# Four hand-written step lists in a graph-attention kernel, put into another order

## The chip, the cores and the metric

The kernel runs on one core of a Trainium2 chip. A time is the device time of one execution in microseconds (us); for a kernel it is the median of the runs shown. The engines are called as in the profile: PE (TensorE's matmuls), PEld (its weight loads), DVE (VectorE), ACT (ScalarE), POOL (GpSimd) and SP (SyncE, which here only issues DMAs).

## What is computed

Two graph-attention layers over 128 batches of 128 nodes with 512 features, all in float32, each with a residual and a layer norm:

```python
# layer 0: 8 heads of 64, masked by adj
q, k, v = x @ Wq + bq, x @ Wk + bk, x @ Wv + bv
logits  = einsum('bqhd,bkhd->bhqk', q, k) / sqrt(64)
attn    = softmax(where(adj > 0, logits, -1e9))
o       = einsum('bhqk,bkhd->bqhd', attn, v)
x       = layernorm(x + relu(o @ Wo + bo))
# layer 1: one head, additive scores, softmax over the senders (axis=1)
Wh = x @ W
e  = leaky((Wh @ a1)[:, :, None] + (Wh @ a2)[:, None, :])
x  = layernorm(x + leaky(softmax(where(adj > 0, e, -9e15), axis=1) @ Wh))
```

## The kernel before

**The order is written out by hand.** The kernel switches the framework's own scheduling off (`tc.manual_schedule`): every engine does its instructions in the order in which the program issues them, and that order stands in strings of tokens. `BEGIN` starts, `PLAN` ends; between them a loop runs t = 6 to 123, 118 times, one batch each, and plays the list `STEADY[t % 4]`. Four lists, 0 to 3, so make one round over a group of four batches, and the loop makes 29.5 rounds. Each token calls one method, which issues a few instructions to one or more engines. In a list, therefore, only the order of tokens that share an engine (or wait for each other) means anything.

**Products.** Q, K and V of a group of four batches (lines 605 to 791) and the products with Wo and W (`pair_product`, line 793, for two batches) use Strassen's scheme: seven products p1 to p7 instead of eight, with sums of blocks before and after. The group products use it twice, one inside the other. The tokens:

- `h`: one of the seven products of a Q, K or V chain, 3 or 4 matmuls of 128x128 (line 681). What has to be read from its PSUM bank goes into two waiting lists: `a` takes the next from the first (a copy by ACT, lines 694 and 697), `d` from the second (an addition by DVE with one operand in PSUM, line 715).
- `k`, `k.v`: one of the 24 sums of two SBUF blocks per group that end the chains (line 731), by POOL or by DVE.
- `q`: one DMA of streamed weights (`w_n`, line 634); four buffers.
- `m.sum.N`, `p.sum.N`, `s.sum.N` (lines 523 to 526): the outer sums before a product, by POOL. `i.s1a` ... `i.s4b` (line 500): the inner ones, by POOL, with `.v` by DVE.
- `z.*`: the product with Wo of two batches, its residual and norm (`LayerZero`); `w.*`: that with W (`LayerOne`). `p1`..`p7` are matmuls (line 801, 0.86 us each), `t0 t2 t3` and `w.c21` copies by ACT, the other `c..` additions by DVE, `by bw` ACT's fill of a bank with the bias.

**Attention of layer 0** (`Softmax`, lines 855 to 980). `f` is the even batch of a pair, `s` the odd one. In lists 0 and 2 both are started: `scores` (line 875) is eight matmuls of 64 rows, which use two halves of the array in turn, and fills two PSUM banks. `add.0 add.1` (889) and `reduce` (898) are DVE's, `exp` (909) and `divide` (923) ACT's, head by head, `reciprocals` DVE's. In lists 1 and 3 both end: `store` (930) writes the weights to DRAM and `fetch` (936) reads them back in another layout, `transpose` (942) is DVE's, `attend` (955) eight matmuls with 64 columns, `copy` (970) four ACT instructions that free its bank.

**Layer 1's attention.** `v.*` and `e.*` (`Senders`, `Edge`; `e.product` is the matmul of line 1211, `e.copy` the ACT instruction of line 1218 that frees its bank and needs that the earlier `n.store`, line 1234, has left the same buffer); `n.*` is the end of the batch before: residual (1221), statistics (1003), `rstd` (POOL, 1009 and 1011), `apply` (DVE, 1024) and the store of the output. `g.*` finishes layer 0's norm of the pair before and fetches it back (421) turned for layer 1.

**Banks.** All matmul results but those of `h` share a pool of five PSUM banks:

```python
ps_mm = ctx.enter_context(tc.tile_pool(name="ps_mm", bufs=5, space=PSUM))
ps_st = ctx.enter_context(tc.tile_pool(name="ps_st", bufs=1, space=PSUM))
```

A new result takes over a bank of the five from an earlier one; PE waits until that one's last reader is done.

Of the kernel before, what the change touches and what calls it, by code (L numbers as in the profile page):

```python
# [70 lines left out]

STEADY = {
    0: """
        k.v n.residual q f.scores h h m.masks m.sum.0 m.sum.1 m.sum.2 m.sum.3 k.v g.apply.0
        q k.v w.p1 f.add.0 f.add.1 g.store.0 e.turn_blocks a e.add m.cast w.t0 s.scores
        f.reduce w.p6 f.exp.0.1 f.exp.2.3 d w.t2 f.exp.4.5 f.exp.6.7 d n.stats s.add.0
        f.reciprocals.0 s.add.1 e.maxima f.reciprocals.1 s.reduce w.p5 h n.rstd w.p7 w.p2 h
        h m.residuals q g.fetch_both a w.t3 e.exp q q w.c22 w.c11 f.divide.2.3 s.exp.2
        f.divide.0.1 a f.divide.6.7 e.divide w.p4 w.p3 h h h w.c21 s.exp.5 v.senders
        f.divide.4.5 s.exp.0.1 a i.s1a.v n.apply d s.exp.6.7 s.exp.3.4 q n.store v.store  # L80
        f.store g.transpose.1 g.transpose.0 i.s3a.v e.product h m.x_pair i.s2a i.s1b m.turn
        d k.v m.mask i.s3b.v a s.reciprocals.0 s.reciprocals.1 w.c12 d i.s2b.v k.v e.copy
        v.fetch
    """,
    1: """
        p.sum.0 z.by n.residual h z.p2 h k h a s.divide.5.6 i.s4a a f.fetch z.p1 h h d
        n.stats n.rstd k.v m.turn e.turn_blocks s.divide.3.4 s.divide.7 s.divide.0.1
        s.divide.2 n.apply z.bw z.t0 h z.p6 z.t2 a m.cast z.p5 z.p7 k k k h z.c11
        f.transpose z.t3 e.add d z.p4 s.store z.c22 a z.p3 h h m.mask e.maxima z.c21 s.fetch
        n.store q e.exp a a d z.stats.1 e.divide i.s4b h e.product h f.attend z.c12 e.copy  # L90
        f.copy p.sum.1 z.rstd.1 p.sum.2 z.apply.1 s.transpose q z.stats.0 d s.attend s.copy
        p.sum.3 z.rstd.0 k k s.sum.2 s.sum.0 s.sum.1 k s.sum.3 m.x_one z.store.1
    """,
    2: """
        f.scores n.residual g.apply.0 w.p1 f.add.1 f.add.0 s.scores e.turn_blocks w.t0 e.add
        w.p6 f.reduce w.t2 w.p2 h w.p7 m.turn k.v k.v f.exp.4.5 f.exp.6.7 f.exp.0.1 k.v w.p5
        h w.t3 a f.exp.2.3 n.stats f.reciprocals.1 w.c22 e.maxima w.c11 f.reciprocals.0
        e.exp f.divide.2.3 n.rstd w.p4 h w.c21 v.senders a d n.apply f.divide.4.5
        f.divide.6.7 f.divide.0.1 e.divide s.add.0 s.add.1 d h w.p3 q g.store.0 m.residuals
        m.masks h e.product h h a a g.fetch_both m.x_one n.store v.store s.reduce  # L100
        g.transpose.0 w.c12 q f.store v.fetch q m.cast d g.transpose.1 m.mask s.exp.5 e.copy
    """,
    3: """
        s.exp.3.4 z.by s.exp.6.7 k.v n.residual n.stats p.sum.0 h f.fetch a s.exp.2 z.p2
        z.p1 h h s.exp.0.1 z.t0 n.rstd q k.v z.p6 p.sum.1 p.sum.2 s.reciprocals.0
        s.reciprocals.1 d s.divide.5.6 a s.divide.0.1 s.divide.7 s.divide.3.4 h
        e.turn_blocks n.apply d z.t2 s.divide.2 m.cast m.turn h a a h z.p7 h h d m.mask
        z.c11 z.bw e.add a z.t3 k k k e.maxima f.transpose k z.p5 q e.exp h h z.p4 h a a d
        z.c22 s.store q q e.divide z.c21 s.fetch z.p3 h d z.stats.1 z.c12 k h n.store
        e.product z.rstd.1 p.sum.3 z.apply.1 d z.stats.0 h h f.attend s.transpose a e.copy a  # L110
        s.attend f.copy s.copy k z.rstd.0 s.sum.0 q z.store.1 s.sum.2 s.sum.1 m.x_one
        s.sum.3
    """,
}

# [1640 lines left out]
```

## Time and profile before

| | us |
|---|---|
| median of 3 runs (2304.18 to 2306.5) | 2305.35 |
| the profiled execution | 2304.29 |
| its span | 2302.5 |
| PE busy | 2265.1 (98%) |
| DVE busy | 2076.6 (90%) |
| ACT busy | 1661.2 (72%) |
| POOL busy | 1443.9 (63%) |
| DMA queue, share of 16 engines' span | 80.3% |

The table's busy times are unions over the span. A matmul's end is modelled, so a busy PE isn't proof of a PE at its peak: for PE, the distance from one start to the next is the number to read. The granted clock of TensorE is full throughout (0.998).

### The profile page before, as it was taken

How to read it: one execution, taken by the hardware profiler on the slowest of the kernel's cores; microseconds unless marked ns; L12 is line 12 of the kernel's file. 1: busy time of each engine (PE TensorE's matmuls, PEld its weight loads, DVE VectorE, ACT ScalarE, POOL GpSimd, SP SyncE). 2: the span in 40 equal slices, each digit the busy share in tenths (PEclk: the TensorE clock that was granted, in tenths of full speed). 3: DMA queues.
4: the chain of work that ended last, by engine and by line, in shares of the span. 5: the costliest groups of instructions: out<-in, count | busy, mean ns of one | idle time of the engine just before them, and what ended most of it. 6: DMA issues, size and time to landing. Idle time of an engine off the chain costs nothing.

```text
span 2302.5 us, 52596 instructions
## 1 busy us (share of the span) xinstructions
PE 2265.1 (98%) x17228; PEld 2013.5 (87%) x17228; DVE 2076.6 (90%) x4199; ACT 1661.2 (72%) x5955; POOL 1443.9 (63%) x1723
## 2 busy tenths in 40 slices
PE   9899999999999999999999999999999999999998
PEld 5889888888898898888988988889889889888885
DVE  5889999999999999999999999999999999999977
ACT  3767767777677677776776776877767767768786
POOL 2666676666766666666667666666666676666656
PEclk9999999999999999999999999999999999999999
DMA  9988888878888888888878888788888788888764
GB/s 234 278 232 233 235 236 243 243 233 228 242 234 251 235 230 237 242 243 239 234 228 243 233 246 241 233 233 242 242 240 237 225 246 235 247 236 233 214 214 144
DMA packets 516593, 540.79 MB, mean 235 GB/s; under 512 B 100568, under 2 KB 394336, under 8 KB 516320
## 3 DMA queue, kind: packets, MB, share of 16 engines
q1 hardware_dynamic: 516000, 537.17, 80.3%
q8 instruction: 137, 2.24, 0.4%
q14 instruction: 136, 1.11, 0.2%
q10 hardware_dynamic: 320, 0.26, 0.0%
HBM read 388.96 MB, written 148.31 MB: 233 GB/s over the span
## 4 chain that ended last, share of the span: by engine, by line
PE 58%; DVE 19%; DMA 9%; POOL 6%; SPq 3%; issue 3%; ACT 2%; DVEq 0%; POOLq 0%; ACTq 0%
PE p_y L801 14%; PE st_y L681 13%; PE lg L875 6%; PE p_w L801 6%; PE st_w L681 6%; PE st_x L681 5%; DVE pa L942 4%; PE p_x L801 4%; DMA w_n<-wv 3%; PE p_oT L955 3%; DVE arena L1047 3%; DVE cells L715 2%; DVE st L1003 2%; PE p_h L1211 2%; DVE arena L1024 2%
## 5 line engine op out<-in xcount | busy, mean ns | idle before, releaser
L909 ACT ACTIVATE pa<-pa,nmax 128x128 f32<-128x128 f32 x1000 | 391.6, 397 | 8.7 <-DVE nmax L898 8.7
L923 ACT ACTIVATE pa<-pa,rs 128x128 f32<-128x128 f32 x1000 | 329.2, 397 | 14.4 <-DVE rs L919 14.3
L1009 POOL TENSOR_SCALAR ve<-mv 128x1 f32<-128x1 f32 x256 | 77.6, 303 | 289.5 <-DVE mv L1005 228.4
L694 ACT COPY cells<-st_y 128x384 f32<-128x384 f32 x279 | 131.7, 472 | 101.4 <-PE st_y L681 98.9
L1024 DVE TENSOR_SCALAR arena<-arena,mv,rstd 128x512 f32<-128x512 f32 x239 | 185.5, 776 | 14.3 <-POOL rstd L1011 14.1
L909 ACT ACTIVATION_READ_ACCUMULATOR pa<-pa,nmax 128x1 f32 x1000 | 194.6, 195 | 0.0
L970 ACT ACTIVATE arena<-p_oT,b_cols 128x128 f32<-128x128 f32 x504 | 144.1, 371 | 58.9 <-PE p_oT L955 54.8
L523 POOL TENSOR_TENSOR x1S<-x1T 128x256 f32<-128x256 f32 x62 | 57.6, 929 | 204.2 <-DVE mf L853 204.2
L1011 POOL TENSOR_TENSOR rstd<-ve,mhalf 128x1 f32<-128x1 f32 x256 | 160.8, 628 | 21.3
L1003 DVE BATCH_NORM_STATS2 st<-arena 128x6 f32<-128x512 f32 x248 | 168.0, 678 | 1.2
L889 DVE TENSOR_TENSOR pa<-lg,mf 128x512 f32<-128x512 f32 x250 | 161.2, 675 | 4.6 <-PE lg L875 4.6
L942 DVE STREAM_TRANSPOSE pa<-paz 128x1024 f32<-128x1024 f32 x125 | 154.5, 1236 | 8.5 <-DMA paz<-pa_dram 6.1
L955 PE MATMUL p_oT<-pa,out_V 128*64 128x128 f32 x2000 | 136.9, 279 | 16.8 <-DVE pa L942 16.8
L875 PEld LDWEIGHTS lg<-out_K,out_Q 64*128 64x128 f32 x2048 | 125.0, 188 | 32.4 <-issue 20.4
L875 PE MATMUL lg<-out_K,out_Q 64*128 64x128 f32 x2048 | 149.4, 286 | 0.7 <-ACT out_K L1395 0.7
L694 ACT COPY out_V<-st_y 128x512 f32<-128x512 f32 x124 | 72.1, 581 | 106.7 <-PE st_y L681 106.5
L898 DVE TENSOR_REDUCE nmax<-pa 128x8 f32<-128x1024 f32 x125 | 148.6, 1189 | 0.1
L955 PEld LDWEIGHTS p_oT<-pa,out_V 128*64 128x64 f32 x2000 | 106.7, 136 | 40.0 <-DVE pa L942 31.2
L1218 ACT ACTIVATE arena<-p_h 128x512 f32<-128x512 f32 x120 | 71.5, 596 | 87.8 <-DMA out_dram<-arena 60.5
L801 PE MATMUL p_y<-wo_w,x1S 128*128 128x257 f32 x496 | 134.3, 393 | 0.2
L801 PE MATMUL p_y<-wo_w,x1T 128*128 128x257 f32 x496 | 132.0, 388 | 0.0
L801 PE MATMUL p_y<-wo_w,oS 128*128 128x256 f32 x504 | 129.8, 380 | 0.4 <-ACT y L812 0.4
(301 smaller groups left out, 7851.7 us busy)
## 6 DMA issues: line engine op xcount, KB each, us to landing
paz<-pa_dram SPq DMA_DIRECT2D x504, 128.0 KB, 3.5
pa_dram<-pa SPq DMA_DIRECT2D x125, 512.0 KB, 3.7
w_n<-wk SPq DMA_DIRECT2D x93, 512.0 KB, 5.5
w_n<-wv SPq DMA_DIRECT2D x93, 512.0 KB, 5.1
w_n<-wk SPq DMA_DIRECT2D x93, 384.0 KB, 4.3
w_n<-wv SPq DMA_DIRECT2D x93, 384.0 KB, 5.0
x_dram<-arena SPq DMA_DIRECT2D x128, 256.0 KB, 2.8
xz<-x_dram SPq DMA_DIRECT2D x240, 128.0 KB, 4.1
```

What stands on the lines that cost most here:

```text
L681: nc.tensor.matmul(p[:, index, :], lhs, rhs, start=start and index == 0, stop=True, skip_group_check=True,)
L694: nc.scalar.copy(dst, p)
L801: nc.tensor.matmul(p[:, :width], xs()[n][:, kc, :], w[:, PLACE[n], kc, :], start=start and kc == 0, stop=True, skip_group_check=True,)
L875: nc.tensor.matmul(self.lg[r][:, c, :], q[rows, 2 * (b % 2) + c % 2, c // 2, :], k[rows, 2 * (b % 2) + c % 2, c // 2, :], start=c == 0, st ...
L889: nc.vector.tensor_add(by_head[:, r * NC : (r + 1) * NC], self.lg[r].rearrange("p c (b k) -> p c b k", b=4), mf.unsqueeze(1).to_broadcast( ...
L909: nc.scalar.activation(self.pa[:, :, h, :], self.pa[:, :, h, :], AF.Exp, bias=self.nmax[:, h : h + 1], accum_out=self.sums[:, h : h + 1],)
L923: nc.scalar.activation(self.pa[:, :, h, :], self.pa[:, :, h, :], AF.Copy, scale=self.rs[:, h : h + 1])
L942: nc.vector.transpose(self.paT.rearrange("p h (a i) -> p a h i", i=32), self.paz.rearrange("p a (h k) -> p a h k", k=32),)
L955: nc.tensor.matmul(self.oT[r * HD : (r + 1) * HD, c, :], v[:, c % 2, c // 2, r * HD : (r + 1) * HD], self.paT[:, r * NC + c, :], start=c == 0,
L1003: nc.vector.bn_stats(st, self.src)
L1011: nc.gpsimd.tensor_tensor(self.r, ve, mhalf, ALU.pow)
L1024: nc.vector.tensor_scalar(self.src, self.src, self.mv[:, 0:1], self.r, ALU.subtract, ALU.mult)
```

## The change

All four lists are written in another order. The functions stay as they are, and the tokens of each list are nearly the same; a few move to the list next to it (`f.fetch` from list 1 to the end of list 0, `s.exp.6.7` from 0 to 1, `s.exp.5` from 2 to 3). In lists 0 and 2 nothing that PE does stands between `f.scores` and `s.scores` any more; `w.p1` follows both. Over the four lists, ten of the 24 sums of line 731 carry `.v` (DVE) where eleven did, and the inner sums of DVE are `s1a s1b s3a` where they were `s1a s3a s3b s2b`. The file is a line shorter, so L801 of before is L800 after.

```diff
 STEADY = {
     0: """
-        k.v n.residual q f.scores h h m.masks m.sum.0 m.sum.1 m.sum.2 m.sum.3 k.v g.apply.0
-        q k.v w.p1 f.add.0 f.add.1 g.store.0 e.turn_blocks a e.add m.cast w.t0 s.scores
-        f.reduce w.p6 f.exp.0.1 f.exp.2.3 d w.t2 f.exp.4.5 f.exp.6.7 d n.stats s.add.0
-        f.reciprocals.0 s.add.1 e.maxima f.reciprocals.1 s.reduce w.p5 h n.rstd w.p7 w.p2 h
-        h m.residuals q g.fetch_both a w.t3 e.exp q q w.c22 w.c11 f.divide.2.3 s.exp.2
-        f.divide.0.1 a f.divide.6.7 e.divide w.p4 w.p3 h h h w.c21 s.exp.5 v.senders
-        f.divide.4.5 s.exp.0.1 a i.s1a.v n.apply d s.exp.6.7 s.exp.3.4 q n.store v.store
-        f.store g.transpose.1 g.transpose.0 i.s3a.v e.product h m.x_pair i.s2a i.s1b m.turn
-        d k.v m.mask i.s3b.v a s.reciprocals.0 s.reciprocals.1 w.c12 d i.s2b.v k.v e.copy
-        v.fetch
+        f.scores m.sum.0 m.sum.2 e.turn_blocks k.v m.sum.1 k.v g.apply.0 n.residual f.add.1
+        f.add.0 s.scores q w.p1 h e.add f.reduce n.stats s.add.0 a w.t0 w.p6 h w.p2 m.turn d
+        e.maxima s.add.1 f.exp.2.3 w.t2 f.exp.0.1 f.exp.6.7 a f.exp.4.5 e.exp w.p7 h m.sum.3
+        s.reduce d h h f.reciprocals.0 e.divide i.s1a.v w.p5 g.store.0 m.residuals m.masks q
+        q n.rstd g.fetch_both w.t3 m.cast a f.divide.2.3 a f.divide.0.1 s.exp.0.1 q d w.c22
+        w.c11 f.reciprocals.1 w.p4 w.c21 v.senders f.divide.6.7 h w.p3 h h n.apply i.s1b.v
+        k.v g.transpose.1 m.mask g.transpose.0 n.store v.store f.divide.4.5 a s.exp.2
+        s.exp.3.4 s.exp.5 i.s2a f.store m.x_pair v.fetch f.fetch e.product h i.s2b a d
+        i.s3a.v s.reciprocals.0 w.c12 d e.copy k i.s3b
     """,
     1: """
-        p.sum.0 z.by n.residual h z.p2 h k h a s.divide.5.6 i.s4a a f.fetch z.p1 h h d
-        n.stats n.rstd k.v m.turn e.turn_blocks s.divide.3.4 s.divide.7 s.divide.0.1
-        s.divide.2 n.apply z.bw z.t0 h z.p6 z.t2 a m.cast z.p5 z.p7 k k k h z.c11
-        f.transpose z.t3 e.add d z.p4 s.store z.c22 a z.p3 h h m.mask e.maxima z.c21 s.fetch
-        n.store q e.exp a a d z.stats.1 e.divide i.s4b h e.product h f.attend z.c12 e.copy
-        f.copy p.sum.1 z.rstd.1 p.sum.2 z.apply.1 s.transpose q z.stats.0 d s.attend s.copy
-        p.sum.3 z.rstd.0 k k s.sum.2 s.sum.0 s.sum.1 k s.sum.3 m.x_one z.store.1
+        z.by s.divide.2 k.v n.residual h h h z.p1 i.s4b i.s4a a s.exp.6.7 z.t0 z.p2 z.p6 d
+        n.stats s.reciprocals.1 a s.divide.0.1 s.divide.3.4 s.divide.7 s.divide.5.6 k.v
+        e.turn_blocks m.turn z.c11 h h h s.store z.t2 e.add z.bw a e.maxima e.exp d
+        f.transpose n.rstd z.p5 z.p7 h q m.x_one s.fetch z.t3 e.divide z.c22 a m.cast z.p4
+        z.c21 n.apply n.store k h h z.p3 m.mask d h z.stats.1 z.c12 q k p.sum.0 k z.rstd.1
+        e.product h d f.attend a a e.copy q s.transpose s.attend z.stats.0 z.apply.1 f.copy
+        s.copy p.sum.2 k k p.sum.1 z.rstd.0 s.sum.0 p.sum.3 k z.store.1 s.sum.2 s.sum.1
+        s.sum.3
     """,
     2: """
-        f.scores n.residual g.apply.0 w.p1 f.add.1 f.add.0 s.scores e.turn_blocks w.t0 e.add
-        w.p6 f.reduce w.t2 w.p2 h w.p7 m.turn k.v k.v f.exp.4.5 f.exp.6.7 f.exp.0.1 k.v w.p5
-        h w.t3 a f.exp.2.3 n.stats f.reciprocals.1 w.c22 e.maxima w.c11 f.reciprocals.0
-        e.exp f.divide.2.3 n.rstd w.p4 h w.c21 v.senders a d n.apply f.divide.4.5
-        f.divide.6.7 f.divide.0.1 e.divide s.add.0 s.add.1 d h w.p3 q g.store.0 m.residuals
-        m.masks h e.product h h a a g.fetch_both m.x_one n.store v.store s.reduce
-        g.transpose.0 w.c12 q f.store v.fetch q m.cast d g.transpose.1 m.mask s.exp.5 e.copy
+        n.residual e.turn_blocks f.scores g.apply.0 f.add.0 f.add.1 s.scores w.p1 e.add w.t0
+        w.p2 w.p6 w.p5 f.reduce e.maxima k f.exp.4.5 e.exp w.t2 w.p7 f.exp.6.7 f.exp.2.3
+        w.t3 m.residuals g.store.0 q m.masks f.exp.0.1 h a h m.turn k.v n.stats e.divide
+        f.reciprocals.1 k.v m.x_one g.fetch_both s.add.1 f.divide.6.7 w.p4 n.rstd w.c21 h
+        n.apply d w.c11 m.cast h w.c22 f.reciprocals.0 v.senders a d e.product h h n.store
+        f.divide.0.1 s.add.0 w.p3 h a f.divide.4.5 s.reduce a f.divide.2.3 v.store q f.store
+        v.fetch e.copy w.c12 g.transpose.1 g.transpose.0 d m.mask
     """,
     3: """
-        s.exp.3.4 z.by s.exp.6.7 k.v n.residual n.stats p.sum.0 h f.fetch a s.exp.2 z.p2
-        z.p1 h h s.exp.0.1 z.t0 n.rstd q k.v z.p6 p.sum.1 p.sum.2 s.reciprocals.0
-        s.reciprocals.1 d s.divide.5.6 a s.divide.0.1 s.divide.7 s.divide.3.4 h
-        e.turn_blocks n.apply d z.t2 s.divide.2 m.cast m.turn h a a h z.p7 h h d m.mask
-        z.c11 z.bw e.add a z.t3 k k k e.maxima f.transpose k z.p5 q e.exp h h z.p4 h a a d
-        z.c22 s.store q q e.divide z.c21 s.fetch z.p3 h d z.stats.1 z.c12 k h n.store
-        e.product z.rstd.1 p.sum.3 z.apply.1 d z.stats.0 h h f.attend s.transpose a e.copy a
-        s.attend f.copy s.copy k z.rstd.0 s.sum.0 q z.store.1 s.sum.2 s.sum.1 m.x_one
-        s.sum.3
+        z.bw p.sum.2 s.exp.2 z.by h z.p1 q s.exp.5 s.exp.6.7 a z.t0 s.exp.0.1 s.exp.3.4 h h
+        z.p6 n.residual n.stats m.turn d s.reciprocals.0 e.turn_blocks s.reciprocals.1 a k
+        p.sum.0 n.rstd k d z.t2 e.add s.divide.3.4 z.p2 h z.p5 h z.c11 s.divide.7 e.maxima
+        s.divide.5.6 s.divide.0.1 s.divide.2 k.v n.apply h m.cast a p.sum.1 z.p7 f.fetch h h
+        a z.t3 e.exp m.x_one q q d f.transpose e.divide z.c22 k k.v a z.p4 h h s.store z.p3
+        h a a k.v k q q h d z.c21 d z.stats.1 h a z.c12 p.sum.3 z.rstd.1 d e.product h h k
+        m.mask z.apply.1 z.stats.0 s.fetch n.store q q s.transpose f.attend s.attend f.copy
+        e.copy s.copy k z.rstd.0 s.sum.2 s.sum.0 s.sum.1 s.sum.3 z.store.1
     """,
 }
```

## The prediction

> **What bounds the kernel now.** The page first, for the bound:
>
> ```profile
> span 2302.5 us, 52596 instructions
> PE 2265.1 (98%) x17228; PEld 2013.5 (87%) x17228; DVE 2076.6 (90%) x4199; ACT 1661.2 (72%) x5955; POOL 1443.9 (63%) x1723
> PEclk9999999999999999999999999999999999999999
> PE 58%; DVE 19%; DMA 9%; POOL 6%; SPq 3%; issue 3%; ACT 2%; DVEq 0%; POOLq 0%; ACTq 0%
> ```
>
> PE is never idle for long, at full clock. So only two things can shorten the steady part: matmuls that follow each other more closely, or fewer waits of PE. Then the waits, for those that PE has:
>
> ```profile
> PE p_oT L955 <- DVE pa L942: 16.8, 60, 2.0
> ACT arena L1218 <- DMA out_dram<-arena: 60.5, 30, 3.3
> POOL ve L1009 <- DVE mv L1005: 228.4, 156, 3.8
> ```
>
> The long ones belong to engines with room. PE's one recurring wait is `s.attend` for `s.transpose`: once per pair of batches. Then PE's timeline over the end of list 1 and the start of list 2, for the distances between starts:
>
> ```profile
> 1115.42 0.39 PE L681 MATMUL st_w<-xS,wq 128*128 128x128 f32 x2
> 1115.74 1.09 PE L955 MATMUL p_oT<-pa,out_V 128*64 128x128 f32 x16
> 1117.08 1.09 PE L955 MATMUL p_oT<-pa,out_V 128*64 128x128 f32 x16 [0.25 <-DVE pa L942]
> 1118.11 1.16 PE L875 MATMUL lg<-out_K,out_Q 64*128 64x128 f32 x16
> 1119.20 1.14 PE L801 MATMUL p_y<-wo_w,x1T 128*128 128x257 f32 x4
> 1120.27 1.16 PE L875 MATMUL lg<-out_K,out_Q 64*128 64x128 f32 x16
> 1121.36 1.14 PE L801 MATMUL p_y<-wo_w,x1S 128*128 128x257 f32 x4
> 1122.33 1.03 PE L801 MATMUL p_x<-wo_w,x1T 128*128 128x257 f32 x4
> 1123.20 0.38 PE L681 MATMUL st_y<-xS,wq 128*128 128x128 f32 x2
> ```
>
> Here the PE is "busy" all along and still loses time. A product undisturbed takes 0.87 us from start to start (1122.33 to 1123.20). `w.p1` between the two score runs takes 1.07, `w.p6` behind the second 0.97, and a run of scores 1.09, though its sixteen starts (two per matmul) alternate 0.007 and 0.105 apart, 0.90 in all. The rest stands at the change from whole-array matmuls to those on a part of the array and back: 0.09 at the last full matmul before, 0.10 at the second pair inside, 0.10 at the exit, 0.10 at the second full matmul after. An isolated run of scores costs 0.39 us over its matmuls.
>
> **The change, step by step.**
>
> *Scores.* In lists 0 and 2 `s.scores` now follows `f.scores` on PE, so per pair one isolated run becomes a continuation, of the same shape and with the usual 0.105 at the joint: 0.39 us less. `f.scores` itself already follows the attends and keeps its price. Even t from 6 to 122 are 59: 59 x 0.39 = 23.0 us, on the path, since PE is the bound. `BEGIN` and `PLAN` are untouched.
>
> What the merged run asks for: four of the five banks at once. The page "TensorEngine Tiling (Array Packing)" of the Trainium skill warns (Gotcha 1) that row tiling raises the pressure on PSUM, which speaks against putting two runs together; it has no price. The trace has: `s.scores` started 2.16 us (list 2) and 3.94 us (list 0) after `f.scores`, and now wants its banks after 1.0. It waits for `f.copy` and `e.copy`, `w.p1` for `s.copy`. Count from the start of `f.attend`: PE reaches `s.attend` at 0.93, `f.scores` at 1.95, `s.scores` at 2.95, `w.p1` at 3.94. On ACT `f.copy` starts 0.17 after its last matmul's end, at 1.27, and lasts 1.16; `e.copy` 0.60 (placed before `f.copy` in list 1, after it in list 3), `s.copy` 1.16; rows of ACT overlap by some 0.1. That gives 2.43, 2.93 and 3.99 in list 3: in time for `s.scores`, 0.05 to 0.1 late for `w.p1`. I charge 0.1 x 59 = 6 us; the ends are 0, and the rival below.
>
> *The wait at `s.attend`.* `s.attend` could start 0.93 after `f.attend`; it starts 1.34 and 1.28 after (the rows above are 1115.74 and 1117.08): a mean of 0.42 in list 1 and 0.38 in list 3 over the trace's rounds, 23.6 us over 59 pairs. What holds `s.transpose` is DVE:
>
> ```profile
> 1114.31 0.69 DVE L1047 SCALAR_TENSOR_TENSOR arena<-y,arena 128x512 f32<-128x512 f32 x1
> 1114.92 0.95 DVE L1024 TENSOR_SCALAR arena<-arena,mv,rstd 128x512 f32<-128x512 f32 x1
> 1115.80 1.23 DVE L942 STREAM_TRANSPOSE pa<-paz 128x1024 f32<-128x1024 f32 x1
> ```
>
> In list 1 `z.apply.1` (0.95) goes behind `s.transpose` and a `d` (0.66) comes ahead; `z.p3`, on which `z.c12` waits, moves 1.56 us closer to `f.attend` on PE (two products `h`, of 0.89 and 0.67, fewer lie between), but `e.divide` and `e.maxima` leave its back. Adding DVE's rows from `z.p3`'s end gives an end of `s.transpose` 3.1 us later; PE needs it after 3.35. In list 3 one more `h` (0.89) stands between `z.p3` and `f.attend`, against 0.2 of `m.mask` moved ahead: 0.7 us gained against a wait of 0.38. So DVE's part of the wait should go in both. Late next is the DMA: `s.store` (3.7 us to landing), then `s.fetch` (3.5). In list 3 its last row landed 0.4 us before `f.attend`, and nothing ahead of it (ACT's `exp` and `divide`, one head more in list 3) gets faster while PE's list does; in list 1 `m.x_one`, four issues (1.8 us of SP, 256 KB, 1.1 us at 235 GB/s), moves ahead of `s.fetch`, which had landed 2.6 us early. Ends: all 23.6 gained, or the wait grown to 0.75 in list 3 (11 us lost). I take half, -12 us.
>
> *VectorE beside GpSimd.* DVE loses one of eleven `k.v` per round (0.67) and about 0.7 of inner sums; POOL gets them (1.3 and 1.0), with 22 of 35 us used per two lists. In the trace `n.residual` takes 0.68 where nothing disturbs it, its row's mean is more, while the `k.v` are nearly free of that already:
>
> ```profile
> L1221 DVE TENSOR_TENSOR arena<-arena 128x512 f32<-128x512 f32 x120 | 97.4, 812 | 1.5 <-ACT arena L1218 1.5
> L731 DVE TENSOR_TENSOR out_K<-out_K,cells 128x512 f32<-128x512 f32 x90 | 60.5, 673 | 0.0
> L731 POOL TENSOR_TENSOR out_K<-out_K 128x512 f32<-128x512 f32 x92 | 115.7, 1272 | 13.2 <-DVE out_K L731 5.3 <-DVE out_K L715 3.2
> ```
>
> "SBUF — State Buffer" of the Trainium skill (Who interferes with whom) says that an addition of two SBUF operands on DVE and a POOL instruction that reads SBUF exclude each other, and the later one blocks fully: up to 1.3 us per addition. By the rule the 120 additions could hold 150 us; by the row it is (0.812 - 0.68) x 120 = 16 us of DVE. I take the row, and at PE zero: DVE's time is covered by PE everywhere but at `s.transpose`, counted above. If that cover goes, it's worth the 16 us at most, either way.
>
> *Queues.* SP: `f.fetch` (four issues) keeps its place behind `v.fetch`; `m.masks` and two `q` of list 0 go behind `g.store.0` and `m.residuals`, so they wait for `n.residual`, some 4 us into the list, and land 5 us later; the product they feed starts about 11 us in: hidden, and 0.39-sized waits if not. `n.store` of list 1 goes far back (rival). POOL: `m.sum`s keep behind `s.sum`s; an extra `k` of K stands before `f.scores` in list 3: two of 1.3 us after a `d` 2.4 us before `f.attend`, done a microsecond before `f.scores`. `i.s1a.v` waits for `m.sum.3` longer, about 0.7 us of idle DVE with 0.5 us left before PE's `w.p3`. I see no other recurring wait of PE, but slacks of 0.2 to 0.5 us in several places; their charge is in the 6 us.
>
> *Sum.* Against the profiled execution (2304.3, its span and 1.8 around it): -23.0 - 12 + 6 = 2275.3; the median lies 1.1 above that execution, so 2276.
>
> **Rivals.**
>
> 1. Everything fits: no new wait, the wait at `s.attend` gone. -23.0 - 23.6: 2259. For it: DVE and ACT have 10 and 28% to spare. Against it: `s.fetch` in list 3.
> 2. Only the scores pay: the `s.attend` wait stays, held by the DMA, and the tight places cost 0.1 per pair: 2305.4 - 23.0 + 6 = 2288.
> 3. Slower: the banks. In list 1 `n.apply` moves behind `z.c21`, so that `n.store` is issued 3.4 to 3.8 us before `f.attend` instead of 5.1; `e.copy` needs its landing and stands ahead of `f.copy` on ACT. At the 3.0 us that L1234 takes in the median it lands just in time. That ACT row does wait for this DMA already, 60.5 us in list 3, where other transfers stood ahead, and `s.fetch` took up to 5.7. At 5.7 here `e.copy` would end 2.6 to 2.9 after `f.attend`'s start, `f.copy` 3.8 to 4.1, and `s.scores`, due at 2.95, would be about 1.0 late in every second pair: 30 us. From a landing of about 5.4 us it eats all that the merge gives; with the 6 us and no gain at `s.attend`: 2305.4 - 23 + 30 + 6 = 2318.
> 4. No change: gain and new waits cancel, 2305.
>
> **How the numbers follow.** Mine 0.50, first rival 0.13, second 0.24, third 0.10, no change 0.03. The time is mine, 2276. The range goes from just under the first rival, 2257, to past the second with 0.15 us more of waits per pair (59 x 0.15 = 9), 2297; beyond lie the third rival and part of "no change". A measurement of this kernel can tell about 0.2%, 4.6 us. Faster 0.87, same 0.03, slower 0.10.
>
> **What would show it.** In PE's timeline two rows of `lg` merge to one of x32, about 2.0 us from its start to the next, and `w.p6` takes 0.87. The second `p_oT` starts under 1.2 us after the first (right) or 1.3 and more (second rival). The waits name `PE lg <- ACT arena L969` or `L1217` if the banks decide (lines are one less). DVE's mean in L1220 under 0.75 would show it kept apart from POOL. The prediction is wrong if PE gets a recurring wait of over 0.4 us per pair anywhere: most likely a product `h` for weights or for a `d`.

## The result, and the profile after

| | before | after |
|---|---|---|
| median of 9 runs each, us | 2306.2 | 2300.8 (2294.9 to 2303.9) |
| ratio, 95% interval | | 0.997 (0.9961 to 0.9979) |
| span of the profiled execution | 2302.5 | 2295.0 |

By the medians the changed kernel is 5.5 us faster (the ratio, 0.997, is one of means), where 29 had been forecast; 2300.8 lies 4 us beyond the upper end of the range. The profiled execution shown here is one of its faster ones. The page:

```profile
span 2295.0 us, 52710 instructions
PE 2250.2 (98%) x17228; PEld 2015.3 (88%) x17228; DVE 2031.0 (89%) x4140; ACT 1654.5 (72%) x5955; POOL 1538.4 (67%) x1782
PEclk9999999999999999999999999999999999999999
PE 58%; DVE 17%; POOL 8%; DMA 8%; ACT 3%; issue 2%; SPq 2%; DVEq 0%; POOLq 0%; ACTq 0%
```

At this scale nothing has changed but POOL's share. PE's timeline over the end of list 1 and the start of list 2 (start, busy us, group) shows what was meant:

```profile
1184.69 0.39 PE L680 MATMUL st_w<-xS,wq 128*128 128x128 f32 x2
1185.01 1.97 PE L954 MATMUL p_oT<-pa,out_V 128*64 128x128 f32 x32
1186.91 2.06 PE L874 MATMUL lg<-out_K,out_Q 64*128 64x128 f32 x32
1188.89 1.14 PE L800 MATMUL p_y<-wo_w,x1T 128*128 128x257 f32 x4
1189.87 0.82 PE L800 MATMUL p_x<-wo_w,x1T 128*128 128x257 f32 x3
```

The two attends follow each other without a pause (one row of 32 matmuls), so do the two runs of scores, and the isolated second run is gone. The waits of PE over the whole execution (us in total, times, longest) say where PE now stands instead:

```profile
PE p_oT L954 <- DVE pa L941: 9.1, 12, 2.2
PE st_y L680 <- DVE out_K L714: 5.6, 12, 0.6
PE st_y L680 <- ACT cells L693: 4.2, 2, 3.8
PE st_y L680 <- DVE cells L714: 2.9, 4, 1.5
```

This view leaves out waits that are shorter than a matmul's modelled end. For those I took each start-to-start distance on PE over t = 12 to 118 (53.5 pairs) and subtracted the undisturbed one for that shape. Three places of the changed kernel carry most of it.

*List 2, `w.p7`: 10.6 us, a wait in every round.* The timeline of all engines there:

```profile
1190.74 1.03 PE L800 MATMUL p_y<-wo_w,x1S 128*128 128x257 f32 x4
1191.06 0.28 DVE L1196 TENSOR_REDUCE nmax<-att 128x1 f32<-128x128 f32 x1
1191.96 0.39 ACT L1200 ACTIVATE att<-att,nmax 128x128 f32<-128x128 f32 x1
1192.35 0.35 ACT L811 COPY arena<-p_y 128x257 f32<-128x257 f32 x1
1192.75 0.92 PE L800 MATMUL p_y<-wo_w,x1S 128*128 128x257 f32 x3
```

Rows 1 and 5 are `w.p6` and `w.p7`, in one bank: `w.p7` adds to what `w.p6` left, so ACT's copy `w.t2` (row 4) must lie between. It stands behind `e.exp` (row 3), and is done at 1192.70. `w.p5`, the product between the two, started at 1191.61; 0.86 later, at 1192.47, PE could have gone on.

*List 3, the fourth `h`: 7.3 us, in 10 of 26 rounds, 0.7 to 0.9 each.* One of them (DVE, POOL, PE):

```profile
1203.23 1.27 POOL L730 TENSOR_TENSOR out_Q<-out_Q,cells 128x512 f32<-128x512 f32 x1
1203.25 1.81 DVE L1220 TENSOR_TENSOR arena<-arena 128x512 f32<-128x512 f32 x1
1206.63 0.65 DVE L714 TENSOR_TENSOR out_K<-st_x,out_K 128x512 f32<-128x512 f32 x1
1207.34 0.49 PE L680 MATMUL st_y<-xT,w_n 128*128 128x128 f32 x2 [0.45 <-DVE out_K L714]
```

POOL's `k` and DVE's `n.residual` started within 0.02 us of each other, and `n.residual` took 1.81 us instead of 0.68. The `d` behind it came late, and PE waited for `d`. `n.residual` of list 3 took 1.80 or 1.81 in 12 of 29 rounds and 0.68 in the others. In those the `k` was the one held up, 1.8 us instead of 1.27, though the starts lie just as close, as here (POOL, DVE):

```profile
1273.37 1.81 POOL L730 TENSOR_TENSOR out_Q<-out_Q,cells 128x512 f32<-128x512 f32 x1
1273.37 0.68 DVE L1220 TENSOR_TENSOR arena<-arena 128x512 f32<-128x512 f32 x1
```

Every round of t = 12 to 118 in which `n.residual` was held up has the wait at the fourth `h`, and no other round has it.

*List 0, the fifth `h`: 5.4 us, in 16 of 27 rounds, about 0.34 each,* for a `d` behind `s.reduce`.

Together they explain the length of a round (from one `f.scores` of list 0 to the next). Before, it was 70.4 us in 21 of 26 rounds, and 70.9 at most. Now it is 69.05 us where only `w.p7` waits, 69.4 with the fifth `h` of list 0, 69.8 with the fourth of list 3, 70.1 with both, and up to 72.1 where `s.attend` of list 3 or another product waits too.

A fourth is paid once, in the first round. The `k` that list 2 gave to POOL stands there behind POOL's work from the beginning:

```profile
142.88 0.71 POOL L730 TENSOR_TENSOR out_Q<-cells 128x256 f32<-128x256 f32 x1
143.62 0.42 DVE L730 TENSOR_TENSOR out_Q<-cells,out_Q 128x256 f32<-128x256 f32 x1 [5.23 <-POOL out_Q L730]
144.16 0.48 ACT L693 COPY cells<-st_y 128x384 f32<-128x384 f32 x1 [4.17 <-DVE out_Q L730]
144.69 0.80 PE L680 MATMUL st_y<-xS,wq 128*128 128x128 f32 x2 [3.82 <-ACT cells L693]
```

DVE, ACT and PE wait in a chain, and that is not all. By stretches (busy time of PE, PEld, DVE, ACT, POOL, then the granted clock, DMA share and GB/s):

```profile
140.50:144.60 4.10, 0.36 (x2) 0.00 (x0) 0.98 (x3) 0.44 (x2) 3.09 (x5) 0.90 0.38 93
144.60:150.60 6.00, 5.91 (x27) 5.91 (x28) 3.63 (x8) 5.16 (x17) 0.00 (x0) 0.50 0.28 91
150.60:156.00 5.40, 5.40 (x42) 5.19 (x41) 3.98 (x9) 4.33 (x20) 2.63 (x4) 1.00 0.76 215
```

After 3.8 us without a matmul PE ran at a granted clock of 0.50 for 6 us. (The first row's 0.90 is a mean: the clock fell at 143.8, before the pause ended.) From the first `f.scores` of the loop to the first `f.attend` it takes 40.1 us, against 34.4 before: 6 us. The page's row of clocks, 57 us to a digit, shows nothing of it.

### The profile page after: what moved, and what is told of

Read it like the earlier page. It is cut to its first block, busy times and chain, and to the rows that moved or that the text cites. A ratio compares the mean times of both kernels' runs of the same rounds, so it can differ in the third digit from the quotient of the medians.

```text
span 2295.0 us, 52710 instructions
## 1 busy us (share of the span) xinstructions
PE 2250.2 (98%) x17228; PEld 2015.3 (88%) x17228; DVE 2031.0 (89%) x4140; ACT 1654.5 (72%) x5955; POOL 1538.4 (67%) x1782
## 4 chain that ended last, share of the span: by engine, by line
PE 58%; DVE 17%; POOL 8%; DMA 8%; ACT 3%; issue 2%; SPq 2%; DVEq 0%; POOLq 0%; ACTq 0%
PE st_y L680 19%; PE p_y L800 13%; PE st_w L680 8%; PE p_w L800 7%; PE st_x L680 4%; DMA paz<-pa_dram 3%; DVE nmax L897 3%; DVE pa L888 3%; PE p_h L1210 2%; PE p_x L800 2%; POOL out_Q L730 2%; POOL rstd L1010 2%; POOL out_K L730 2%; PE lg L874 2%; ACT pa L908 1%
## 5 line engine op out<-in xcount | busy, mean ns | idle before, releaser
L524 POOL TENSOR_TENSOR x1S<-x1T 128x256 f32<-128x256 f32 x62 | 48.7, 786 | 245.6 <-PE st_y L680 237.3
L1010 POOL TENSOR_TENSOR rstd<-ve,mhalf 128x1 f32<-128x1 f32 x256 | 189.7, 741 | 21.3
L1008 POOL TENSOR_SCALAR ve<-mv 128x1 f32<-128x1 f32 x256 | 82.2, 321 | 129.3 <-DVE mv L1004 127.7
L714 DVE TENSOR_TENSOR cells<-st_w,cells 128x384 f32<-128x384 f32 (+1 forms) x217 | 123.2, 568 | 44.2 <-ACT cells L693 41.6
L1023 DVE TENSOR_SCALAR arena<-arena,mv,rstd 128x512 f32<-128x512 f32 x239 | 143.7, 601 | 14.0 <-POOL rstd L1010 14.0
L730 POOL TENSOR_TENSOR out_Q<-out_Q,cells 128x512 f32<-128x512 f32 x91 | 131.6, 1447 | 15.4 <-DVE out_Q L730 9.9
L954 PE MATMUL p_oT<-pa,out_V 128*64 128x128 f32 x2000 | 127.6, 278 | 9.2 <-DVE pa L941 9.1
L800 PE MATMUL p_y<-wo_w,x1S 128*128 128x257 f32 x496 | 131.1, 386 | 3.9 <-ACT arena L811 0.2
L874 PE MATMUL lg<-out_K,out_Q 64*128 64x128 f32 x2048 | 133.8, 280 | 0.7 <-ACT out_K L1394 0.7
L800 PE MATMUL p_y<-wo_w,x1T 128*128 128x257 f32 x496 | 134.4, 393 | 0.0
L730 POOL TENSOR_TENSOR out_K<-out_K 128x512 f32<-128x512 f32 x32 | 53.7, 1681 | 115.6 <-PE st_x L680 107.0
L800 PE MATMUL p_y<-wo_w,oS 128*128 128x256 f32 x504 | 129.7, 380 | 0.5 <-ACT y L811 0.5
```

Of the source, the lines that this page charges most:

```text
L730: (by or engine).tensor_add(*(t(n) for t, n in (dst, left, right)))
L800: nc.tensor.matmul(p[:, :width], xs()[n][:, kc, :], w[:, PLACE[n], kc, :], start=start and kc == 0, stop=True, skip_group_check=True,)
L874: nc.tensor.matmul(self.lg[r][:, c, :], q[rows, 2 * (b % 2) + c % 2, c // 2, :], k[rows, 2 * (b % 2) + c % 2, c // 2, :], start=c == 0, st ...
L1010: nc.gpsimd.tensor_tensor(self.r, ve, mhalf, ALU.pow)
L1023: nc.vector.tensor_scalar(self.src, self.src, self.mv[:, 0:1], self.r, ALU.subtract, ALU.mult)
```

## The experiments

The theory: the merge is worth its 0.39 us per pair on PE, and new waits of PE gave most of that back. The rival: another engine's chain sets the length of a round, and the merge is worth nothing. The kernel before ran beside each of them, at a median of 2306.3 to 2307.4. "Waits" and "rest" are PE's over t = 12 to 118, as above, with 0.105 us at the second matmul behind a run of scores counted to the rest, since it belongs to the price of that run. They come from one profiled execution each, which lies up to 6 us from the kernel's median, so a few us of waits more or less decide nothing. The medians come from four occasions, each with its own runs of before.

| kernel | median, us | ratio to before, 95% | waits | rest |
|---|---|---|---|---|
| before | 2306 | | 24 | 1857 |
| after | 2300.8 | 0.9961 to 0.9979 | 33 | 1834 |
| 1 merge alone in before | 2338.6 | 1.0124 to 1.0153 | 72 | 1837 |
| 2 after, not merged | 2305.1 | 0.9983 to 1.0001 | 17 | 1855 |
| 3 after, four moves | 2299.9 | 0.9957 to 0.9981 | 43 | 1834 |
| 4 after, one `k` by DVE | 2296.3 | 0.9947 to 0.9970 | 39 | 1834 |
| 5 merge in before, with cover | 2317.1 | 1.0036 to 1.0060 | 54 | 1837 |
| 6 after, `n.rstd` first | 2290.6 | 0.9914 to 0.9939 | 29 | 1834 |
| 7 after, four better moves | 2286.9 | 0.9898 to 0.9923 | 22 | 1834 |
| 8 as 7, `h` as cover | 2287.5 | 0.9894 to 0.9925 | 28 | 1834 |
| 9 after, `z.apply.1` first | 2304.2 | 0.9979 to 0.9996 | 42 | 1834 |
| 10 as 7, `a` first | 2275.3 | 0.9847 to 0.9873 | 17 | 1834 |
| 11 as 7, not merged | 2295.9 | 0.9937 to 0.9966 | 17 | 1855 |

**The rest column is the merge by itself.** It is 1855 to 1857 in the three kernels with isolated scores and 1834 in eight of the ten with merged ones (1837 in the two made from before): 21.6 us over 53.5 pairs, 0.40 us a pair, where the prediction read 0.39 from one timeline. It doesn't depend on the rest of the order. So all else that these kernels differ in is waits, and the start.

**1. The merge alone.**

```diff
 0:  -k.v n.residual q f.scores h h m.masks m.sum.0 ... k.v g.apply.0 q k.v w.p1 ... w.t0 s.scores f.reduce w.p6
     +k.v k.v k.v n.residual q f.scores s.scores h h m.masks m.sum.0 ... g.apply.0 q w.p1 ... w.t0 f.reduce w.p6
 2:  -f.scores n.residual g.apply.0 w.p1 f.add.1 f.add.0 s.scores
     +f.scores s.scores n.residual g.apply.0 w.p1 f.add.1 f.add.0
```

> The kernel before with one part of the change: in lists 0 and 2 s.scores directly behind f.scores on PE (three k.v that Q needs go ahead of it in list 0); all else in the order of before. Theory (an isolated run of scores costs 0.39 us on PE and the merge saves it 59 times; the rest of the change gave most of it back through new waits of PE): 2306 - 23 = 2283, and up to 2295 if the four banks or the three earlier k.v make waits of 0.2 us per pair; the two rows of lg become one of x32 and w.p6 takes 0.87. Rival (the length of a round is set by the way over s.store, s.fetch and s.transpose to s.attend, and what PE saves comes back as a longer wait there): within 5 us of 2306, with the waits of p_oT for pa grown from 17 us to some 40.

2338.6: 32 slower than before, which neither theory had. The rival's sign, longer waits for `pa`, is missing (14.9 us, as against 16.8). The new wait, and one instance of it:

```profile
PE p_y L801 <- ACT arena L812: 33.1, 59, 0.6
1212.17 1.14 PE L801 MATMUL p_y<-wo_w,x1T 128*128 128x257 f32 x4
1213.34 0.38 ACT L812 COPY arena<-p_y 128x257 f32<-128x257 f32 x1 [1.90 <-PE p_y L801]
1213.86 1.11 PE L801 MATMUL p_y<-wo_w,x1S 128*128 128x257 f32 x4 [0.56 <-ACT arena L812]
```

`w.p6` adds to the bank of `w.p1` and needs ACT's copy `w.t0` in between. From start to start that takes 1.7 us, of which PE has 0.9 to do. In the order of before the second run of scores stood in this gap. It cost 0.39 us of its own, and it was the cover for 0.7 us. 44 us of waits at `w.p6` over t = 12 to 118 answer to it.

**2. The changed kernel with the scores apart.**

```diff
 0:  -f.add.0 s.scores q w.p1 h         +f.add.0 w.p1 s.scores q h
 2:  -f.add.0 f.add.1 s.scores w.p1     +f.add.0 f.add.1 w.p1 s.scores
```

> The changed kernel with s.scores put back behind w.p1 in lists 0 and 2, so that both runs of scores are isolated again; all else as changed. Theory (merge worth 0.39 us per pair on PE, the rest of the change a net loss): 2301 + 23 = 2324, slower than both kernels, down to 2312 if the waits that the change made at w.p7 and at two h shrink by what PE loses ahead of them. Rival (the merge is worth nothing because another chain sets the round): 2301.

4 us over the changed kernel. The 21 us come back in the rest, and 15 of them leave the waits: `w.p7` goes from 10.6 to 0.8 us, the fifth `h` of list 0 from 5.4 to nothing. In this order these two waits exist only with the merge. So the whole merge is worth 4 us here (the two intervals of the ratio don't overlap): nearer the rival's 2301 than the theory's 2312, though not for the rival's reason.

**3. Four moves at once.**

```diff
 0:  -s.reduce d h h                    +d s.reduce h h
 2:  -e.maxima k f.exp.4.5 e.exp w.t2   +e.maxima k.v f.exp.4.5 w.t2 e.exp
 3:  -z.p6 n.residual n.stats m.turn d  +z.p6 d n.residual n.stats m.turn
```

> The changed kernel with the places put back that I hold for its new waits: list 2's early k by DVE instead of POOL (start, 6 us), w.t2 ahead of e.exp on ACT (10.6 us at w.p7), d ahead of n.residual on DVE in list 3 (7.3 us at h), d ahead of s.reduce in list 0 (5.4 us at h). Theory (these are PE's own losses and nothing else is as late): 2301 - 29 = 2272. Rival (each is the first of several waits close behind one another; who is freed waits at the next place): 2290 or more, with new rows of PE waits of the same sum.

2299.9, as the rival had it. The waits at the three old places fell to under 2 us each, and two others came up: 18.5 us at the seventh `h` of list 3, 7.0 at the third of list 2. The first:

```profile
1207.78 2.14 ACT L922 ACTIVATE pa<-pa,rs 128x128 f32<-128x128 f32 x7
1210.39 0.57 ACT L693 COPY out_K<-st_y 128x512 f32<-128x512 f32 x1
1211.01 0.49 PE L680 MATMUL st_w<-xS,w_n 128*128 128x128 f32 x2 [0.38 <-ACT out_K L693]
```

PE no longer waits at the fourth `h`, but ACT's copy stands behind seven divides, which need DVE's `s.reciprocals`, and these stand behind `n.residual`. My move put the `d` ahead of it, and a `d` has to wait for its product: in this round DVE stood idle for 1.54 us before it, and `n.residual`, now at 0.68, started 1.3 us later than in the changed kernel. The place was right and the remedy wrong.

**4. The start alone.**

```diff
 2:  -e.maxima k f.exp.4.5              +e.maxima k.v f.exp.4.5
```

> The changed kernel with only list 2's first k done by DVE (k.v). Theory (at the first round this k stands behind POOL's work from the beginning; DVE, ACT and PE wait for it, PE is idle for 3.8 us and its clock then halves for 6 us): -6 from the changed kernel, 2295, and the granted clock near the span's 145 us stays at full. Rival (the late start is made up, since the round's length is set elsewhere; or the DVE, 89% busy, pays 0.67 us per round for the extra addition, 20 us in all): 2301 to 2310.

4.5 us faster than the changed kernel by the medians, which alone would not be clear of the noise: the two intervals of the ratio overlap. The trace is clearer. The stretch at 145 us is at full clock, and from the first `f.scores` to the first `f.attend` it takes 33.3 us instead of 40.1. In all six kernels with this `k` by DVE (3, 4, 7, 8, 10, 11) it takes 33.3 to 34.7 us, in the four with it by POOL (the changed one, 2, 6, 9) 38.6 to 40.1.

```profile
145.00:150.00 5.00, 4.94 (x38) 4.59 (x38) 4.49 (x8) 5.00 (x20) 1.43 (x3) 1.00 0.74 231
```

**5. The merge in before, with something in the gap.** To the first experiment:

```diff
 0:  -f.scores s.scores h h ... a e.add m.cast w.t0 f.reduce w.p6
     +f.scores s.scores h ...   e.add m.cast w.t0 h a f.reduce w.p6
 2:  -w.t0 e.add w.p6 f.reduce w.t2 w.p2 h w.p7
     +w.t0 e.add w.p2 w.p6 f.reduce w.t2 h w.p7
```

> The merge alone in the list order of before, as in the first experiment, but with another product put where s.scores stood between w.p1 and w.p6: an h in list 0 (its copy a follows it), w.p2 in list 2. Theory (the first experiment lost 44 us at w.p6 because the score run of 1.1 us had covered ACT's copy w.t0 between w.p1 and w.p6; with another cover the 0.39 us per pair come through): round 70.41 - 0.8 = 69.6 us, 2306 - 23 = 2283, up to 2292 if w.p7 or h wait a little; no wait of p_y for arena. Rival (the merge is worth nothing on PE, or DVE's chain sets the round): 2301 to 2306 with the waits of p_oT for pa grown.

2317: 21 us better than without cover, the wait at `w.p6` is gone, and still 11 slower than before. The saved time turned into shorter waits at many places: 9.1 us at `w.p7` of list 0, 7.3 and 4.6 at two `h` of list 2, 3.5 at its `w.p7`. So with the merge PE arrives earlier at many places whose order was set for a later one. That most of the other moves in the changed lists answer to this is my reading; no run takes them one by one.

**6. POOL out of `n.residual`'s way.**

```diff
 3:  -s.reciprocals.1 a k p.sum.0 n.rstd k   +s.reciprocals.1 a n.rstd k p.sum.0 k
```

> The changed kernel with one move on POOL: in list 3 n.rstd goes ahead of one k and of p.sum.0, so that POOL does no addition while DVE does n.residual there. Theory (an addition of DVE beside one of POOL is held up by up to 1.1 us, from 0.68 to 1.81, and DVE's d and with it PE's h come late by up to 0.8 in two rounds of three): n.residual of list 3 at 0.68, the wait of st_y for out_K gone, 7 to 10 us less: 2291 to 2294. Rival (ACT's copies a behind the divides, which ended last when d was put ahead, are the next wait): the wait moves by three products and the time stays at 2299 to 2301.

10 us faster than the changed kernel, as the theory said; but the wait it removes had stood in 10 rounds of 26 there, not in two of three. `n.residual` of list 3 takes 0.68 in all 29 rounds, and the wait of `st_y` for `out_K` is gone. The row of the groups (count, busy us, mean ns) was 95.4 and 795 in the changed kernel and is now:

```profile
L1220 DVE TENSOR_TENSOR arena<-arena 128x512 f32<-128x512 f32 x120 | 82.5, 687 | 1.5 <-ACT arena L1217 1.5
```

**7 and 8. The remedies together; another cover for `w.p7`.** Seven is the third with the sixth's move in place of `d` ahead of `n.residual`. Eight differs from seven in list 2:

```diff
 2:  -f.exp.4.5 w.t2 e.exp w.p7 ... f.exp.0.1 h a h
     +f.exp.4.5 e.exp w.t2 h w.p7 ... f.exp.0.1 a h
```

> The changed kernel with list 2's first k on DVE, w.t2 ahead of e.exp, d ahead of s.reduce in list 0, and n.rstd ahead of k and p.sum.0 in list 3, in place of d ahead of n.residual, which moved the wait to ACT's a (18.5 us at the seventh h of list 3). Theory (four separate waits of PE, and only the one in list 3 was mended at the wrong place): 2300 - 18 (h of list 3) + 7 (its wait gone, nothing in its place) ... worked out as 2301 - 4 - 10 - 5 - 8 + 7 (the third h of list 2, which then waits for a) = 2281. Rival (every place freed only moves the wait on): 2292 to 2300.

> As the kernel with the four moves of this call, but w.p7 of list 2 keeps e.exp ahead of w.t2 and gets an h ahead of it instead (0.89 us of PE work in place of the score run that stood there before the merge). Theory (w.p7 lacks cover, 0.4 us per round): no wait at w.p7 and none at the third h of list 2, 7 us less than the other: 2274. Rival (ACT, with six more rows in that stretch than PE gives it time for, ends last in either order): same as the other within 3 us.

2286.9 and 2287.5: better than both kernels, and no more than the fourth and sixth moves add up to (4.5 + 10.2). The waits at `w.p7` (2.2 and 0.5 us) and in list 0 are all but gone, yet 6.8 to 7.3 us stand at the third `h` of list 2, for ACT's copy `a`. So the eighth's rival was right; the seventh lies between its theory's 2281 and its rival's 2292. The moves at `w.p7` and in list 0 were not run one by one.

**10. That copy.** To the seventh:

```diff
 2:  -f.exp.0.1 h a h                   +h a f.exp.0.1 h
```

> The kernel with the four moves that measured 2287, and in list 2 the copy a ahead of f.exp.0.1 on ACT. Theory (the third h of list 2 waits for this a, 0.25 us per round; f.exp.0.1 has over 0.6 us left until f.reciprocals.0 needs it): 7 us less, 2280. Rival (w.p4 and w.c11 behind it, or the divides, become late): 2285 to 2288.

2275.3, 32 us faster than the kernel before beside it (2307.4). That is 11.6 us under the seventh, where the wait removed was 6.8. The two profiled executions differ by 5.8, and the seventh's was the fastest of its five; what the rest of the 11.6 is stays open. The three longest rows of PE's waits:

```profile
PE p_oT L954 <- DVE pa L941: 6.7, 9, 2.5
PE st_y L680 <- DVE cells L714: 4.6, 7, 0.7
PE st_w L680 <- DMA w_n<-wv: 1.9, 5, 0.6
```

**11. The merge's worth once the waits are mended.** The seventh with the second's edit:

> The kernel with the four moves that measured 2287, and s.scores put back behind w.p1 in lists 0 and 2. In the changed kernel the same step back cost only 4 us. Theory (the merge is worth 23 us of PE time; in the changed kernel the waits that came with it, 16 us at w.p7 and at an h of list 0, took most of it, and these two are now mended; what is left of waits that a score run in between would cover is the third h of list 2, 7 us): 2287 + 16 = 2303, up to 2310. Rival (the merge is worth 4 us wherever it stands, since DVE's or ACT's order sets the round): 2291.

2295.9: the same step back that cost 4 us in the changed kernel costs 9 here, against the seventh; neither the theory's 16 nor the rival's 4. Against the tenth it is 20.6, but that one has a move more; what the tenth would lose without the merge was not run.

**9. `z.apply.1` back ahead of `s.transpose`.**

```diff
 1:  -q s.transpose s.attend z.stats.0 z.apply.1   +q z.apply.1 s.transpose s.attend z.stats.0
```

> The changed kernel with z.apply.1 put back ahead of s.transpose in list 1. Theory (DVE held s.attend; with z.apply.1 of 0.8 us ahead, s.transpose, which ends 0.33 us before PE needs it, ends 0.45 late): a wait of 0.45 us per round at s.attend in list 1, 13 us: 2314. Rival (that wait went for another reason, the later f.attend or earlier DMA): 2301.

The wait at `s.attend` of list 1 returns in all 27 rounds, 0.27 us in the median and 9.7 in sum. In all but one `s.transpose` starts without a pause of DVE behind `z.apply.1`, so it was DVE's; in the one, the DMA came last (1.6 us). Another 3.6 us came at `s.attend` of list 3, while `w.p7` and the fifth `h` of list 0 gave back 6.9, since PE arrives there later. By the medians the time rises by 3.4 us, by the two profiled executions by 10 (2305.0 against 2295.0); the theory's 13 did not come either way. What a wait costs is not its length, as what a merge saves is not its price.

## Why the prediction was wrong

**The merge, -23.0: right** as PE's own time. 0.40 us a pair, in every kernel. As time of the kernel it came through only in part, 4 us in the second experiment and 9 in the eleventh, since waits came with it; they belong to the third term.

**The wait at `s.attend`, -12: right, a little small.** It was 21.4 us over 53.5 pairs and is 5.5: none in list 1, and 12 rounds of list 3. Scaled to 59 pairs, -17.5. The ninth shows that the reason given, `z.apply.1` ahead of `s.transpose`, held for list 1; for list 3 no run tests it. I had taken half because of the DMA. It does hold `s.attend` in just those 12 rounds: DVE stands idle before `s.transpose` in each of them, 0.3 to 1.8 us, and a DMA ends that. The row for the whole execution:

```profile
DVE pa L941 <- DMA paz<-pa_dram: 12.4, 19, 1.7
```

So the mechanism was right, and the DMA's share was a quarter instead of half.

**New waits, +6: the step that failed.** PE's waits other than `s.attend` went from 2.7 to 27.2 us over t = 12 to 118, which is +27 on 59 pairs. With the first two terms and the 6 us at the start: -23.7 - 17.5 + 27 + 6 = -8, against -5.5 by the medians, -6.9 by the means and -7.5 by the two profiled executions. Three readings are behind it:

- I costed a run of scores as PE's time alone, and looked for who *it* would wait for (the banks). I did not ask who had used it as cover. 16 of the 27.2 us, at `w.p7` and at the fifth `h` of list 0, come of this. The places were in front of me: `w.p1`, `w.p6` and `w.p7` share a bank, with an ACT copy between each. The prediction put such places down as "slacks of 0.2 to 0.5 us in several places" and charged 0.1 per pair for `w.p1` in their stead.
- I weighed a mean over a row against a rule, and took the mean. "SBUF — State Buffer" of the Trainium skill (Who interferes with whom) says that two such instructions exclude each other, and the later one fully waits. The 0.812 us of before were no average of mild disturbance: 0.68 in lists 0 to 2 and 1.22 in all 29 rounds of list 3. (Rows of both stand below.) The rule held for the single instance, nearly in full (1.81 for the two together, where 1.27 and 0.68 add up to 1.95), and the sixth shows what it cost. "At PE zero" was wrong too: the `d` behind had 0.5 us of slack in the changed kernel (it ends 0.57 before its product starts where nothing disturbs it, 0.06 where PE waits for it), and `n.residual` was late by 1.1. This made the 7.3 us.
- Of the first round I wrote that `BEGIN` is untouched. But the first play of a list met queues that are not those of the steady loop: there one `k` moved to POOL cost 6 us.

`n.residual` of before in lists 2 and 3 of one round, for the second of these:

```profile
1188.76 0.68 DVE L1221 TENSOR_TENSOR arena<-arena 128x512 f32<-128x512 f32 x1
1204.18 1.22 DVE L1221 TENSOR_TENSOR arena<-arena 128x512 f32<-128x512 f32 x1
```

**The rivals.** The third, slower by the banks through `n.store`, did not come: `lg` waits nowhere in the loop. The measured time lies between the second and "no change". The second's reason failed, since most of the attend wait did go. That of "no change", gain and new waits cancelling, I gave a chance of 0.03, and it came nearest: 41 us of gain against 33 of new waits and start. Of the signs that I had named, the row of x32 came, and so did waits at "a product `h` for weights or for a `d`"; but none of over 0.4 us a pair, as I had set the mark: it is the sum of several, 0.46 a pair, that did it. DVE's mean under 0.75 did not come (0.795).

## What to carry to other kernels

An instruction that PE could do without may be the cover for a hand-over between other engines: before it is moved, list what runs beside it, above all copies between two matmuls into one bank. When a saving on the critical engine is real, the next wait stands close behind: read who is second to last, and mend the places until the sum of waits, not one of them, has fallen. And take a row's mean apart by place before it enters a sum: 0.81 us was the duration of no instruction.

## What the runs showed of the hardware

The pause of PE of 3.8 us at the start was followed by 6 us at a granted clock of 0.50; together they cost about 6 us. The same pause in the second, sixth and ninth kernel (3.82 and 3.83 us) was followed by about 3 us at 0.50, so the pause alone doesn't settle the length. "TensorE: Matmul & The Clock Gate" of the Trainium skill (Why this matters for your kernels) advises against pauses of over about 3 us. Here shorter ones could do it too: near its end the kernel before has a pause of 1.97 us (from 2207.5, by the modelled ends), and from 2210.2 on 3.4 us at 0.50, so its clock isn't quite full throughout. And a pause of 2.88 us near the end of the eleventh kernel had no slow stretch behind it.

Two additions, one by DVE and one by POOL, that start within 0.02 us of each other took 0.68 and 1.8 us or 1.81 and 1.27: one of them is held up, in 12 rounds DVE's and in 17 POOL's. The recorded starts don't tell which. Only where it is DVE's does PE wait. The changed kernel's executions also spread more, 2294.9 to 2303.9 against 2304.2 to 2308.9; that this is why is not shown, and the seventh kernel, where `n.residual` of list 3 is no longer held up in this way, spreads as widely (2280.8 to 2290.1).
